# Layer 0 of a graph network on one core: order of the last chunks, filler products in PE's waits, a fifth search behind the scaling, and one gather for the last tile's neighbours

## The chip, the cores and the metric

The kernel runs on one core of a Trainium2 chip. The metric is the device time of one execution in microseconds. The engines are named as the profile names them: PE multiplies matrices (its weight loads are PEld), DVE does vector work, ACT activations and copies, POOL issues the gathers, SP issues most transfers.

## The reference, cut to what matters

Four layers work on x (2708 nodes, 128 features) and a weighted adjacency matrix adj (2708 x 2708, fp32). The change is in layer 0:

```python
def _lap_mul(A, x):
    d = 1.0 / jnp.sqrt(jnp.sum(A, axis=-1))
    return d[:, None] * (A @ (d[:, None] * x))
...
z = _lap_mul(A, x) @ W1 + b1
z = jax.nn.leaky_relu(z, negative_slope=0.1)
sq = jnp.sum(z * z, axis=-1)
d2 = sq[:, None] + sq[None, :] - 2.0 * (z @ z.T)
d2 = jnp.maximum(d2, 0.0)
S = jnp.exp(-jnp.sqrt(d2 + 1e-10) / (2.0 * sigma))
S = jnp.where(ranks < k, S, 0.0)   # the k = 4 nearest nodes of each row
A2 = S + A
out = _lap_mul(A2, x) @ W2 + b2
...
h = jnp.maximum(_layernorm(x, axis=-1), 0.0)
x = x + _L0_gnn_ref(h, adj, L0_gnn_W1, L0_gnn_b1, L0_gnn_W2, L0_gnn_b2, 1, 4)
```

So layer 0 multiplies by adj twice, once with the degrees of adj, and once with those of adj plus a sparse matrix of four neighbours a row. Layers 1 to 3 (attention, a mean aggregation, a plain one) follow with the new x.

## The kernel before, in words

**Tiles and chunks.** The nodes are cut into 22 tiles of 128 rows (T = 22), the last of 20 (TAIL), in six groups of four (GROUPS). adj lies transposed in DRAM. A chunk is 128 of its rows by 2708 columns, 1354 KB, the last 20 rows by 2708, 212 KB. `chunk(i)` (L80 to L90) loads chunk i by a transfer on SP's queue into one of the four buffers of the pool "big", or, for the last five (L0_RES = 5: chunks 17 to 21), into slots res17 to res21 of the pool "rows", where they stay. A product over all nodes is six column blocks, five of 512 and one of 148, in six PSUM tiles acc0 to acc5. PE does an fp32 product in two passes, so a chunk makes 12 records.

**Stage 1, sums** (loop at L366 to L381). While chunks 0 to 21 stream in, PE sums the columns of each with a 32-column matrix of ones (L373), and between them, in `weighted` (L335 to L362), transposes the normalised x and multiplies it by W1 and W2. The sums become degrees and their inverse roots (L382 to L406), which scale y1 (L410).

**Stage 2, aggregation 1** (`aggregate`, L272 to L316). For each streamed chunk, six column blocks times y's tile (`product`, L284); the resident chunks come last, block by block, and after each block `done` uses the result. The last 20 rows are loaded three times more at other partitions (`last_rows`, L92 to L99).

**Stage 3, strips** (L504 to L535). For each tile PE makes z times z transposed, with the squares added by a bf16 product (L520); ACT copies each PSUM tile to a strip of 128 x 2708 in SBUF (L527); DVE finds the eight largest of each row (`max`, L529) and their places (`max_index`, L531). For the last four tiles (LATE = T - 4) the places are put off (`find_last`, L547): two of their strips live in the slots U and Z of the pool "lay", two in "big". Then the distances of the four nearest become similarities on ACT and DVE, new degrees and dinv2 (L552 to L569), and y2 is scaled, tile by tile, by DVE and ACT (L574 to L579) and written to DRAM (ydr) in two parts of 11 tiles (L581 to L586). Behind that on DVE stand the four put-off searches (L590), and `row_numbers` (L541), which turns places into rows of ydr (near_u).

**Stage 4, aggregation 2 and neighbours** (L748 to L758). `add_near` (L600 to L617) does, for each tile and each of the four neighbours, an indirect gather on POOL of 128 rows of ydr into one of 23 buffers, and on DVE a term: gathered rows times the similarity, added to xs. Tiles 0 to 14 are recorded ahead of aggregation 2, tiles 15 to 19 in `done_l0` (L733) after group results, tiles 20 and 21 at the end. Aggregation 2 on y2 keeps chunks 13 to 16 in their buffers (kept=4). The tail adds the last tiles' terms, normalises the last group and goes on to layer 1.

**What sets the order.** Each engine runs its instructions in one order. A scheduler places what isn't pinned (`pin`), pools decide which buffer a tile gets, and a transfer or a writer waits until the buffer's last reader has finished. Transfers on SP and ACT take one of eight lanes in turn, and a transfer waits for the one before it on its lane. Transfers on SP are pinned to program order, so one that waits holds up those behind it.

Of the kernel before, what the change touches and what calls it, by code (L numbers as in the profile page):

```python
# [9 lines left out]
F32 = mybir.dt.float32  # L10
U32 = mybir.dt.uint32
BF16 = mybir.dt.bfloat16
AF = mybir.ActivationFunctionType
ALU = mybir.AluOpType
# [4 lines left out]
P = 128  # L19
TOPK = 4  # L20
# [5 lines left out]
def kernel(  # L26
# [18 lines left out]
    nc = tc.nc  # L45
    N, D = x.shape
    assert D == P
    T = -(-N // P)
    TAIL = N - (T - 1) * P
    KBS = [(k0, min(512, N - k0)) for k0 in range(0, N, 512)]  # L50
    NKB = len(KBS)
    GROUPS = [(t, min(t + 4, T)) for t in range(0, T, 4)]
    L0_RES = 5
    TAIL_RES = 6

    def width(t):
        return TAIL if t == T - 1 else P
# [8 lines left out]
    lay = ctx.enter_context(tc.tile_pool(name="lay", bufs=1))  # L66
# [3 lines left out]
    ps_s = ctx.enter_context(tc.tile_pool(name="ps_s", bufs=2, space=PSUM))  # L70
    ps_a = ctx.enter_context(tc.tile_pool(name="ps_a", bufs=1, space=PSUM))

    def pin(ins):

        return tc.keep_in_program_order(ins)

    resident = {}
# [24 lines left out]
    def spread(y, queue):  # L102

        for g in range(1, 4):
            queue.dma_start(y[32 * g : 32 * g + TAIL, T - 1, :], y[:TAIL, T - 1, :])
# [4 lines left out]
    res_rows = rows_open.enter_context(tc.tile_pool(name="rows", bufs=1))  # L110
    pools.update(res=res_rows, n=L0_RES)
    xs = keep.tile([P, T, D], F32, name="xs")
# [9 lines left out]
    ident = consts.tile([P, P], F32, name="ident")  # L122
# [25 lines left out]
    with nc.allow_non_contiguous_dma(reason="256 elements"):  # L148
# [3 lines left out]
    ident_b = consts.tile([P, P], BF16, name="ident_b")  # L152
# [20 lines left out]
        out=tri, in_=ones_b, pattern=[[-1, P]], compare_op=ALU.is_ge, fill=0.0, base=0, channel_multiplier=1  # L173
# [23 lines left out]
    def acc(b):  # L197
        return ps_a.tile([P, 512], F32, name=f"acc{b}")

    def span(g):  # L200
        return slice(GROUPS[g][0] * P, min(GROUPS[g][1] * P, N))

# [69 lines left out]
    def aggregate(y, done, more=None, kept=0, back=1, first=1):  # L272

        out = [acc(b) for b in range(NKB)]
        last = T - pools["n"]

        def product(i, b):
            k0, n = KBS[b]
            r = slice(32 * (b % 4), 32 * (b % 4) + TAIL) if i == T - 1 else slice(0, P)
            nc.tensor.matmul(  # L284
                out[b][:, :n],
                y[r, i, :],
                chunk(i)[r, k0 : k0 + n],
                start=(i == 0),
                stop=(i == T - 2),
            )  # L290

        for i in range(last):
            if more is not None:
                more(i)
            resident[i] = chunk(i)
            if i > 2 and T - 1 in resident and pools["apart"]:
                last_rows()
            for b in range(NKB):
                product(i, b)
            if i < last - kept:  # L300
                del resident[i]
            if i >= back and (i - back) % 2 == 0:
                absent = [j for j in range(last, T) if j not in resident]
                for j in absent[: first if i == back else 1]:
                    chunk(j)
        if more is not None:
            for i in range(last, T):
                more(i)
        for b in range(NKB):
            product(T - 1, b)  # L310
        for b in range(NKB):
            for i in range(last, T - 1):
                product(i, b)
            if b:
                done(b - 1, out)
        done(NKB - 1, out)  # L316

    NG = len(GROUPS)
# [5 lines left out]
    res = l0.enter_context(tc.tile_pool(name="l0_res", bufs=1))  # L324
# [10 lines left out]
    def weighted(g, part):  # L335
        t0, t1 = GROUPS[g]
        if part == 0:
            p = acc(g % 2)
            for t in range(t0, t1):
                o = (t - t0) * P  # L340
                mm = nc.tensor.transpose(
                    p[:, o : o + width(t)], h0[: width(t), t, :], ident[: width(t), : width(t)]
                )
                if t == t0:
                    pin(mm)
            nc.scalar.copy(h0T[:, span(g)], p[:, : span(g).stop - span(g).start])
            return
        dst, w = ((y1, w1), (hw2, w2))[part - 1]
        p = acc(2 * part + g % 2)
        for t in range(t0, t1):  # L350
            o = (t - t0) * P
            mm = nc.tensor.matmul(
                p[: width(t), o : o + P], h0T[:, cols(t)], w, start=True, stop=True
            )
            if t == t0:
                pin(mm)
        for a, e, n in ((t0, min(t1, T - 1), P), (max(t0, T - 1), t1, TAIL)):
            if a < e:
                (nc.scalar.copy, nc.vector.tensor_copy)[part - 1](
                    dst[:n, a:e, :],  # L360
                    p[:n, (a - t0) * P : (e - t0) * P].rearrange("p (t f) -> p t f", f=P),
                )  # L362

    for g in range(NG):
        layernorm_relu(h0, g)
    for i in range(T):  # L366
        c = chunk(i)
        w = width(i)
        if 3 <= i < 3 + 3 * NG:
            weighted((i - 3) // 3, i % 3)  # L370
        for b, (k0, n) in enumerate(KBS):
            g = 32 * (b % 4)
            nc.tensor.matmul(  # L373
                sums[b // 4][g : g + 32, :n],
                ones[:w, :32],
                c[:w, k0 : k0 + n],
                start=(i == 0),
                stop=(i == T - 1),
            )
        if i < FIRST:  # L380
            del resident[i]  # L381
    sum_rows = lay.tile([P, 1024], F32, name="sum_rows", tag="U")  # L382
    for half, p0, p1 in ((0, 0, 128), (1, 0, 32 * (NKB - 5)), (1, 32 * (NKB - 5), 32 * (NKB - 4))):
        n = KBS[4 * half + p0 // 32][1]
# [3 lines left out]
    for g0, g1 in [(0, 4)] + [(b, b + 1) for b in range(4, NKB)]:  # L388
# [3 lines left out]
        for c in range(min(4, e - 4 * g0)):  # L392
            w = min(width(4 * b + c) for b in range(g0, g1))
# [84 lines left out]
    p = ps_s.tile([P, 512], F32, name="ps")  # L478
    pin(nc.tensor.transpose(p[:, :P], wg, ident))
    nc.vector.tensor_copy(wgT, p[:, :P])  # L480
    p = ps_s.tile([P, 512], F32, name="ps")
# [10 lines left out]
    top_v = res.tile([P, T, 8], F32, name="top_v")  # L492
    top_i = res.tile([P, T, 8], U32, name="top_i")

    LATE = T - 4
    strips = []
    nc.vector.memset(top_v[:, T - 1, :], 0.0)

    def strip(t):
        if LATE <= t < LATE + 2:  # L500
            return lay.tile([P, N], F32, name=f"strip{t}", tag="UZ"[t - LATE])
        return big.tile([P, N + 1], F32, name="strip", tag="big")[:, :N]

    for t in range(T):  # L504
        w = width(t)
# [3 lines left out]
        for bs in (range(4), range(4, NKB)):  # L509
            for b in bs:  # L510
                k0, n = KBS[b]
# [5 lines left out]
            for b in bs:  # L517
                k0, n = KBS[b]
                g = 32 * (b % 4)
# [4 lines left out]
                    start=False,  # L524
                    stop=True,
# [12 lines left out]
    near_u = res.tile([P, T, TOPK], U32, name="near_u")  # L538
# [28 lines left out]
    dinv2 = keep.tile([P, T], F32, name="dinv2")  # L567
    nc.scalar.activation(deg2s, deg2s, AF.Ln)
    nc.scalar.activation(dinv2, deg2s, AF.Exp, scale=-0.5)  # L569
    y2 = lay.tile([P, T, D], F32, name="y2", tag="Y")  # L570
    ydr = dram.tile([P * T, D], F32, name="ydr")
    for i in range(2):
        resident[i] = chunk(i)
    for t0, t1 in ((0, T // 2), (T // 2, T)):  # L574
        for t in range(t0, t1):
            if t % 5 in (1, 3):
                scaled = nc.scalar.mul(y2[:, t, :], hw2[:, t, :], dinv2[:, t : t + 1])
            else:
                nc.vector.tensor_scalar(  # L579
                    y2[:, t, :], hw2[:, t, :], dinv2[:, t : t + 1], None, op0=ALU.mult  # L580
                )  # L581
        pin(
            nc.sync.dma_start(
                ydr.rearrange("(p t) f -> p t f", t=T)[:, t0:t1, :], y2[:, t0:t1, :]
            )
        )  # L586
    with tc.issue_after(scaled.ins):
        nc.scalar.preload_act_table_set("sqrt_and_others")
    for t in (T - 2, T - 1, *range(LATE, T - 2)):
        find_last(t)  # L590
# [4 lines left out]
    simd = res.tile([P, T, TOPK], F32, name="simd")  # L595
    nc.vector.tensor_tensor(
        simd, sim, dinv2[:, :, None].to_broadcast([P, T, TOPK]), ALU.mult
    )

    def add_near(t, late=False):  # L600
        w = width(t)
        for k in range(TOPK):
            g = res.tile([P, D], F32, name="gath", bufs=23)
            nc.gpsimd.indirect_dma_start(  # L604
                out=g[:w, :],
                out_offset=None,
                in_=ydr[:, :],
                in_offset=bass.IndirectOffsetOnAxis(ap=near_u[:w, t, k : k + 1], axis=0),
            )
            term = nc.vector.scalar_tensor_tensor(  # L610
                xs[:w, t, :],
                g[:w, :],
                simd[:w, t, k : k + 1],
                xs[:w, t, :],
                op0=ALU.mult,
                op1=ALU.add,
            )  # L617
            if late and k == 0:
                pin(term)
# [127 lines left out]

    for t in range(15):  # L748
        add_near(t)
    aggregate(y2, done_l0, lambda i: spread(y2, nc.sync) if i == 4 else None, kept=4)  # L750
    transposed(hT, h1, NG - 2, nc.scalar.copy)
    column_terms(NG - 3)
    for t in range(GROUPS[-1][0], T):
        add_near(t, late=True)
    layernorm_relu(h1, NG - 1)
    last_row = last_terms(NG - 1)
# [248 lines left out]
    p = acc(0)  # L1005
# [94 lines left out]
    for t in range(T):  # L1100
# [3 lines left out]
        for b, (k0, n) in enumerate(EKBS):  # L1104
            p = acc(b)
# [272 lines left out]
```

## Time and profile before

| What | us |
|---|---|
| Median of five runs | 1286.74 |
| The five runs | 1278.62, 1291.21, 1277.50, 1289.09, 1286.74 |
| Profiled execution: its time | 1287.12 |
| Profiled execution: span, first to last instruction | 1285.3 |
| PE busy in the span | 1055.8 (82%) |
| Mean granted PE clock | 0.902 of full |
| Stage 1 ends (first product of aggregation 1) | 93.39 |
| Strips: PE | 205 to 327.5 |
| First product of aggregation 2 | 337.06 |
| First and last gather of the long run of gathers | 343.99 and 448.1 |
| Aggregation 2 ends | 528 |
| Layer 0 ends | about 552 |

The page shows the span in 40 slices of 32 us, each digit a tenth of busy time; PEclk is the clock that PE was granted. In the groups, the number after the second bar is how long the engine stood idle just before, and what ended it; "issue" means that the profile shows nothing that it waited for. In a timeline a row has start, duration, engine, line, operation, and idle time before it in brackets. Some matmul records are missing, a few in a hundred.

### The profile page before, as it was taken

Reading aid. Unit: us, or ns where it says so; the run is one execution under the profiler, and the core shown is the slowest. Engines: PE = TensorE matmul, PEld = TensorE weight load, DVE = VectorE, ACT = ScalarE, POOL = GpSimd, SP = SyncE. Lnnn points to the kernel's source line nnn. Section 1 sums busy time; section 2 is a strip of 40 time slices with the busy share of each in tenths; the row PEclk is TensorE's granted clock in tenths of the full one; section 3 lists DMA queues with packets and bytes.
Section 4 is the critical chain, followed back from the end, with each engine's and each line's share of the span. In section 5 each row is a group of like instructions: output and inputs, shape, how many; then the busy total and the mean of one; then the engine's idle time right before and its main releaser. Section 6 shows DMA issues by size and latency. Waiting matters only on the chain. (4 is left out here: it accounts for less than half of the span.)

```text
span 1285.3 us, 10181 instructions
## 1 busy us (share of the span) xinstructions
PE 1055.8 (82%) x3603; PEld 498.4 (39%) x3603; DVE 561.0 (44%) x1177; ACT 410.2 (32%) x636; POOL 243.5 (19%) x211
## 2 busy tenths in 40 slices
PE   3879999999763379798677861787879999999998
PEld 1324444444220134454333430333334445545444
DVE  2020026999932001783566663899970022104003
ACT  3100014544300000475567744687840012003000
POOL 4000000000277700134211103576500000000000
PEclk9989999999875579778899996688889999999999
DMA  9997800001553361256999986999949945761841
GB/s 339 421 388 281 302 2 1 1 1 43 209 206 96 94 247 56 90 226 253 270 401 397 346 360 255 422 422 418 417 180 400 334 162 185 263 244 56 307 157 43
DMA packets 38801, 298.76 MB, mean 232 GB/s; under 512 B 6736, under 2 KB 9711, under 8 KB 12291
## 3 DMA queue, kind: packets, MB, share of 16 engines
q1 hardware_dynamic: 24798, 203.76, 42.0%
q0 software_dynamic: 13952, 94.36, 19.6%
q8 instruction: 28, 0.46, 0.1%
q14 instruction: 23, 0.18, 0.0%
HBM read 265.76 MB, written 32.87 MB: 232 GB/s over the span
## 5 line engine op out<-in xcount | busy, mean ns | idle before, releaser
L284 PE MATMUL acc<-chunk,y 128*128 128x512 f32 (+1 forms) x408 | 180.7, 592 | 74.1 <-issue 59.4
L1213 PE MATMUL acc<-hi,xw 128*128 128x512 f32 (+3 forms) x264 | 123.9, 633 | 57.8 <-DVE hi L1203 57.8
L1106 PE MATMUL acc<-mov,wt 128*128 128x512 f32 (+1 forms) x264 | 115.7, 592 | 40.3 <-DMA mov<-in_adj_dram,src_u 40.0
L284 PE MATMUL acc<-chunk,h 128*128 128x512 f32 (+1 forms) x384 | 148.3, 542 | 0.0
L604 POOL DMA_INDIRECT gath<-ydr,near_u x88 | 83.8, 952 | 337.3 <-DMA ydr<-y 245.8
L284 PEld LDWEIGHTS acc<-chunk,y 128*128 128x128 f32 x408 | 79.3, 204 | 175.4 <-issue 164.5
L512 PE MATMUL acc<-zT 128*128 128x512 f32 (+2 forms) x264 | 112.7, 559 | 0.4 <-ACT strip L527 0.3
L1213 PEld LDWEIGHTS acc<-hi,xw 128*128 128x128 f32 (+1 forms) x264 | 55.5, 219 | 126.2 <-issue 66.0
L1110 DVE COPY mov<-acc 2x512 f32<-2x512 f32 x126 | 74.1, 611 | 59.9 <-PE acc L1106 59.5
L284 PEld LDWEIGHTS acc<-chunk,h 128*128 128x128 f32 x384 | 68.6, 190 | 73.2 <-issue 73.1
L1106 PEld LDWEIGHTS acc<-mov,wt 128*128 128x128 f32 x264 | 52.1, 205 | 103.5 <-issue 91.1
L527 ACT COPY strip<-acc 128x512 f32<-128x512 f32 (+2 forms) x132 | 60.7, 556 | 61.0 <-issue 35.8
L284 PE MATMUL acc<-chunk,attended 128*128 128x512 f32 x192 | 73.1, 542 | 1.2 <-DMA chunk<-in_adj_dram 1.2
L1111 ACT COPY knots<-acc 128x512 f32<-128x512 f32 x88 | 50.5, 590 | 62.1 <-DVE mov L1110 54.1
L1145 POOL DMA_INDIRECT lo<-table,lo_u x22 | 56.1, 2549 | 71.8 <-issue 41.5
L1195 ACT ACTIVATE hi<-hi,lam 128x2708 f32<-128x2708 f32 (+3 forms) x24 | 56.5, 2363 | 34.7 <-issue 25.3
L1191 DVE SCALAR_TENSOR_TENSOR hi<-lo,lam,hi 128x2708 f32<-128x2708 f32 (+3 forms) x24 | 67.1, 2801 | 1.0
L1203 DVE SCALAR_TENSOR_TENSOR hi<-row_all,inv_s,hi 128x2708 f32<-128x2708 f32 (+3 forms) x24 | 67.0, 2797 | 0.4 <-ACT hi L1196 0.4
L512 PEld LDWEIGHTS acc<-zT 128*128 128x128 f32 (+1 forms) x264 | 45.0, 185 | 51.7 <-issue 41.9
L529 DVE MAX8 top_v<-strip 128x8 f32<-128x2708 f32 (+1 forms) x22 | 64.4, 2967 | 0.4 <-ACT strip L527 0.4
L650 ACT COPY u2T<-acc 128x512 f32<-128x512 f32 (+1 forms) x6 | 3.2, 532 | 168.2 <-PE acc L284 168.1
L1196 ACT ACTIVATE hi<-hi,hb 128x2708 f32<-128x2708 f32 (+3 forms) x24 | 56.5, 2361 | 0.7
(281 smaller groups left out, 1177.2 us busy)
## 6 DMA issues: line engine op xcount, KB each, us to landing
chunk<-in_adj_dram SPq DMA_DIRECT2D x108, 1354.0 KB
table<-knots SPq DMA_DIRECT2D x20, 1354.5 KB
res<-in_adj_dram SPq DMA_DIRECT2D x9, 1354.0 KB
chunkY<-in_adj_dram SPq DMA_DIRECT2D x2, 1354.0 KB
chunkU<-in_adj_dram SPq DMA_DIRECT2D x2, 1354.0 KB
res<-in_adj_dram SPq DMA_DIRECT2D x8, 211.6 KB
ydr<-y SPq DMA_DIRECT2D x2, 704.0 KB
gath<-ydr,near_u POOLq DMA_INDIRECT x88
```

What stands on the lines that cost most here:

```text
L284: nc.tensor.matmul(out[b][:, :n], y[r, i, :], chunk(i)[r, k0 : k0 + n], start=(i == 0), stop=(i == T - 2),)
L512: mm = nc.tensor.matmul(zz[b][:w, :n], zT[:, cols(t)], zT[:, k0 : k0 + n], start=True, stop=False)
L527: copied = nc.scalar.copy(s[:w, k0 : k0 + n], zz[b][:w, :n])
L529: nc.vector.max(top_v[:w, t, :], s[:w, :])
L604: nc.gpsimd.indirect_dma_start(out=g[:w, :], out_offset=None, in_=ydr[:, :], in_offset=bass.IndirectOffsetOnAxis(ap=near_u[:w, t, k : k + ...
L1106: nc.tensor.matmul(p[:, :n], wt[:, t, :], moving[t][:, k0 : k0 + n], start=True, stop=True)
L1110: nc.vector.tensor_copy(moving[t + 1][:2, k0 : k0 + n], p[:2, :n])
L1191: nc.vector.scalar_tensor_tensor(num, lo[:w, c], kap, num, op0=ALU.mult, op1=ALU.add)
L1195: nc.scalar.activation(num, num, AF.Ln, scale=sc)
L1196: nc.scalar.activation(num, num, AF.Exp, scale=-1.0, bias=hb40[:w, t : t + 1])
L1203: nc.vector.scalar_tensor_tensor(att[:w, c], row_all[:w, c], inv_s[:w, t : t + 1], att[:w, c], op0=ALU.max, op1=ALU.mult,)
L1213: nc.tensor.matmul(py[b][:, :n], xw[:w, t, :], att[:w, k0 : k0 + n], start=(t == T - 1), stop=(t == T - 2),)
```

## The change

Six edits, all in layer 0.

1. The sums take chunks 0 to 19, then 21 (20 rows), then 20. The transfers on SP change places in the same way.
2. A function `warm(p, n)` issues n bf16 products of 128 x 512 whose result nobody reads. Three follow each of the last six chunks of the sums, into acc0; sixteen stand after the strips and ahead of aggregation 2, into acc5. In PE's order the sixteen come directly behind the last strip's products, and wait only for ACT's copies of acc5.
3. LATE = T - 5: tile 17's search is put off too. Its strip takes the slot of the resident chunk 17, so aggregation 2 loads that chunk again, behind chunk 7's load on SP (back=7). That load waits for the search of strip 17. DVE has five searches in place of four behind y2.
4. ydr is written in three parts, of 9, 8 and 5 tiles.
5. The 4 x 20 neighbours of the last tile are gathered at once: eight copies of 20 x 1 on ACT's queue lay their row numbers and similarities out on four groups of partitions (near_p, simd_p), one gather of 128 rows fetches them, and a product on PE with four_w (sums of blocks of the identity, scaled by simd_p) adds the four groups up; DVE adds the result to xs. 85 gathers in place of 88. On POOL this gather is the 81st, ahead of tile 20's four; on DVE the scaling of four_w stands behind the 32nd of the 60 terms that go ahead of aggregation 2's group results. ACT's eight copies stand behind its table load after y2.
6. In the tail tile 21 goes ahead of tile 20.

The diff, cut to its core:

```diff
+    def warm(p, n):
+        for _ in range(n):
+            pin(
+                nc.tensor.matmul(
+                    p, ident_b, ident_b[:, None, :].to_broadcast([P, 4, P]), start=True, stop=True
+                )
+            )
...
-    for i in range(T):
+    for n_, i in enumerate([*range(T - 2), T - 1, T - 2]):
...
-                start=(i == 0),
-                stop=(i == T - 1),
+                start=(n_ == 0),
+                stop=(n_ == T - 1),
...
+        if n_ >= T - 6:
+            warm(acc(0), 3)
...
-    LATE = T - 4
+    LATE = T - 5
...
-        if LATE <= t < LATE + 2:
-            return lay.tile([P, N], F32, name=f"strip{t}", tag="UZ"[t - LATE])
+        if t == LATE:
+            i = T - L0_RES
+            del resident[i]
+            return res_rows.tile([P, N + 1], F32, name=f"strip{t}", tag=f"res{i}")[:, :N]
+        if LATE < t < LATE + 3:
+            return lay.tile([P, N], F32, name=f"strip{t}", tag="UZ"[t - LATE - 1])
...
+    warm(acc(5), 16)
...
-    for t0, t1 in ((0, T // 2), (T // 2, T)):
+    for t0, t1 in ((0, 9), (9, 17), (17, T)):
...
+    near_p = res.tile([P, 1], U32, name="near_p")
+    simd_p = res.tile([P, 1], F32, name="simd_p")
...
+    for k in range(TOPK):
+        for dst, src in ((near_p, near_u), (simd_p, simd)):
+            nc.scalar.dma_start(dst[32 * k : 32 * k + TAIL, :], src[:TAIL, T - 1, k : k + 1])
+    four_w = res.tile([P, 32], F32, name="four_w")
+    nc.vector.tensor_tensor(four_w, ident[:, 0:32], ident[:, 32:64], ALU.add)
+    nc.vector.tensor_tensor(four_w, four_w, ident[:, 64:96], ALU.add)
+    nc.vector.tensor_tensor(four_w, four_w, ident[:, 96:128], ALU.add)
...
+        if t == T - 1:
+            g = gathered(near_p)
+            nc.vector.tensor_scalar(four_w, four_w, simd_p, None, op0=ALU.mult)
+            p = ps_s.tile([P, 512], F32, name="ps")
+            nc.tensor.matmul(p[:TAIL, :P], four_w[:, :TAIL], g, start=True, stop=True)
+            nc.vector.tensor_tensor(xs[:TAIL, t, :], xs[:TAIL, t, :], p[:TAIL, :P], ALU.add)
+            return
...
-    aggregate(y2, done_l0, lambda i: spread(y2, nc.sync) if i == 4 else None, kept=4)
+    aggregate(y2, done_l0, lambda i: spread(y2, nc.sync) if i == 4 else None, kept=4, back=7)
...
-    for t in range(GROUPS[-1][0], T):
+    for t in reversed(range(GROUPS[-1][0], T)):
```

More of the change, by code (lines that the diff above doesn't have):

```diff
@@ L365 @@
         layernorm_relu(h0, g)
[L366 removed]
+    for n_, i in enumerate([*range(T - 2), T - 1, T - 2]):
         c = chunk(i)
         w = width(i)
[L369 to L370 removed]
+        if 3 <= n_ < 3 + 3 * NG:
+            weighted((n_ - 3) // 3, (n_ - 3) % 3)
         for b, (k0, n) in enumerate(KBS):
@@ L598, with gathered @@
     )
-    def add_near(t, late=False):
-        w = width(t)
-        for k in range(TOPK):
[L603 to L609, printed above, removed]
+    near_p = res.tile([P, 1], U32, name="near_p")
+    simd_p = res.tile([P, 1], F32, name="simd_p")
+    nc.vector.memset(near_p, 0)
+    nc.vector.memset(simd_p, 0.0)
+    for k in range(TOPK):
[5 more added lines that the diff above has]
+    nc.vector.tensor_tensor(four_w, four_w, ident[:, 96:128], ALU.add)
+    def gathered(idx):
+        g = res.tile([P, D], F32, name="gath", bufs=23)
+        nc.gpsimd.indirect_dma_start(
+            out=g[: idx.shape[0], :],
+            out_offset=None,
+            in_=ydr[:, :],
+            in_offset=bass.IndirectOffsetOnAxis(ap=idx, axis=0),
+        )
+        return g
+    def add_near(t, late=False):
+        if t == T - 1:
[5 more added lines that the diff above has]
+            return
+        for k in range(TOPK):
+            g = gathered(near_u[:, t, k : k + 1])
             term = nc.vector.scalar_tensor_tensor(
[L611 to L614, printed above, removed]
+                xs[:, t, :],
+                g,
+                simd[:, t, k : k + 1],
+                xs[:, t, :],
                 op0=ALU.mult,
```

## The prediction, made before the changed kernel ran

> **What bounds the kernel now.** I read the page's slices first, then its costliest groups, a table of stages by windows, and the timelines at the seams that the diff touches. From the page:
>
> ```profile
> PE   3879999999763379798677861787879999999998
> PEclk9989999999875579778899996688889999999999
> DMA  9997800001553361256999986999949945761841
> ...
> L284 PE MATMUL acc<-chunk,y 128*128 128x512 f32 (+1 forms) x408 | 180.7, 592 | 74.1 <-issue 59.4
> L604 POOL DMA_INDIRECT gath<-ydr,near_u x88 | 83.8, 952 | 337.3 <-DMA ydr<-y 245.8
> ```
>
> PE is near full except in slices 10 to 16 (320 to 550 us). The two aggregations on L284 waited 59.4 us for "issue", for nothing that the profile names. The table of windows (us, busy us and records of each engine, granted clock, DMA share, GB/s) places it:
>
> ```profile
> 80.00:84.70 4.70, 2.29 (x16) 0.65 (x8) 0.48 (x2) 0.00 (x0) 0.00 (x0) 1.00 1.00 270
> 84.70:90.00 5.30, 5.26 (x24) 0.95 (x24) 0.65 (x1) 0.00 (x0) 0.00 (x0) 0.68 1.00 412
> 93.40:100.00 6.60, 6.60 (x10) 2.83 (x11) 2.63 (x5) 0.00 (x0) 1.57 (x3) 0.61 0.63 220
> ...
> 327.50:337.00 9.50, 0.00 (x0) 0.00 (x0) 7.77 (x12) 2.82 (x10) 0.00 (x0) 0.67 0.27 109
> 337.00:344.00 7.00, 6.93 (x13) 3.23 (x14) 7.00 (x17) 3.75 (x10) 0.01 (x1) 0.72 0.66 232
> 344.00:368.00 24.00, 23.99 (x64) 11.18 (x62) 12.96 (x29) 0.00 (x0) 18.26 (x19) 1.00 0.85 332
> 368.00:412.00 44.00, 13.98 (x17) 4.40 (x16) 12.21 (x35) 0.00 (x0) 33.29 (x36) 0.54 0.31 86
> 412.00:456.00 44.00, 14.98 (x18) 4.82 (x17) 2.73 (x8) 0.00 (x0) 27.59 (x29) 0.50 0.32 106
> ```
>
> The reader is to see four seams: a DMA dip to 270 GB/s at 80; clocks of 0.68 and 0.61 after it; PE empty from 327.5 to 337 while DVE searches; and from 368 to 456 only 35 products in 88 us, with DMA a third busy and POOL gathering throughout. In the PE timeline the products of the last stretch stand 2.8 us apart, though 76 of them ran in 31.4 us just before:
>
> ```profile
> 337.06 31.38 PE L284 MATMUL acc<-chunk,y 128*128 128x512 f32 x76 [9.60 <-DVE y L579]
> ...
> 400.49 1.01 PE L284 MATMUL acc<-chunk,y 128*128 128x512 f32 x1 [1.78 <-issue]
> 403.29 1.01 PE L284 MATMUL acc<-chunk,y 128*128 128x512 f32 x1 [1.80 <-issue]
> ```
>
> I call this the slow stretch. 35 products at 0.41 us are some 14 us of the 88, so it costs about 74 us. SP's waits there are named "remote": PE's releases of chunk buffers reach it late as well.
>
> ```profile
> SPq L87 <- remote: 83.0, 3, 33.2
> ```
>
> Its cause isn't in the profile. In time it goes with POOL: gathers run back to back, 0.95 us plus 0.30 of gap, from 343.99 to 448, and PE is quick again from 456. The burst is 83 gathers: 60 whose terms DVE adds at once (done at 421), and 23 that fill the buffers. So whatever moves the first gather moves the end of the stretch, and whatever PE does before the stretch is kept.
>
> **The change part by part**, against the profiled execution (1287.1 us; the median of five runs is 1286.7, its range 1277.5 to 1291.2).
>
> 1. *Order of the last chunks, three unread products after each of the last six.* Before:
>
> ```profile
> 79.64 1.90 PE L373 MATMUL ps<-res,ones 128*32 128x512 f32 x12 [0.61 <-DMA res<-in_adj_dram]
> 84.74 5.38 PE L373 MATMUL ps<-res,ones 128*32 128x512 f32 x24 [2.45 <-DMA res<-in_adj_dram]
> ```
>
> Twelve records take 1.90 us at full clock; the last 24 took 5.38, 1.6 over, as the clock had dropped while PE waited for chunk 20. It landed at 84.7 (5.1 us after chunk 19 instead of 3.25), the 20 rows at 86.1. The bytes stay the same, so with the order turned round the full chunk lands between 84.7 and 86.1 and is followed by one set of 1.90 us and three unread products. Those: a strip tile takes 5.58 us, its twelve fp32 passes 4.55 of that, so 2708 bf16 columns take 1.03 and 512 take 0.2 us; 0.6 per chunk. In the busiest of these rounds PE then has 1.90 + 1.16 + 0.6 = 3.7 us against 3.25 of load, a lag under 1 us that the lighter rounds after it make good. The sums end at 88 to 89 instead of 90.1: -1.2. The first aggregation ran at half clock from 92.0 to 98.9, some 5.5 us of its own work, 2.7 lost; the products end only 1.5 us nearer to it, so I take half of that, -1.5. Together **-2.7**, ends 0 (the load still lands at 86.1 and the clock drops anyway) and -4.5. After it PE is continuous to 180, so it is kept.
>
> 2. *One more search put off.* Each search is 2.97 us plus 0.08 on DVE, which lags ACT at the end of the strips:
>
> ```profile
> 331.18 2.96 DVE L529 MAX8 top_v<-strip 20x8 f32<-20x2708 f32 x1
> ...
> 339.35 2.97 DVE L549 FIND_INDEX8 top_i<-top_v,strip 128x8 uint32<-128x2708 f32 x1
> ```
>
> ACT's last strip copy ends at 328.7, so the last maximum can start 2.5 us earlier, not 3.05: **-2.5**, ends 0 and -3.05. The search comes back after y2: five there instead of four, first term of DVE at about 3 us later against y2. That is covered: 23 buffers are 23 x 1.25 = 29 us of gathers. Chunk 17 is loaded once more (1354 KB, 3.25 us) behind chunk 7 on SP; in the windows from 368 DMA is at a third, so 0. If that cover went it is at most 3.25 us.
>
> 3. *Sixteen unread products ahead of aggregation 2.* They wait for ACT's last strip copy: 328.7 on before's clock, 16 x 0.2 = 3.2 us, end 331.9, and the first y2 product comes at 337.06 - 2.5 = 334.6. PE stood at half clock from 330.96 to 341.2, 3.5 us after its last product; of that, 4.1 us was work, so 2.07 us was lost. The new gap is 2.7 us, under 3.5: the clock stays. At half clock they take 6.4 us and end at 335.1: 0.5 late. I take -2.07, ends +0.5 and -2.07. The page "TensorE: Matmul & The Clock Gate" of the Trainium skill (Part 1) has the clock fall after an idle window of about 3.4 us, the window running freely; the row's 3.5 agrees. By a free-running window a gap of 2.7 us could now and then still fall in one: without the gain of the clock the sum would be -6.1 in place of the -8.2 below.
>
> 4. *y2 to DRAM in three parts.* The two parts were issued at 338.26 and 339.49 and landed at 341.4 and 343.1, the first gather came at 343.99. With a smaller last part I take **-0.8** for the first gather, ends 0 and -1.5. SP's one more issue stands ahead of chunk 2's, half a microsecond that the next loads hide.
>
> 5. *Last tile's neighbours in one gather.* Eight copies of 20x1 on ACT's queue, which was idle from 340.8 to 506. Three such 20-row copies took SP 2.44 us to issue at 344.3, so eight are 6.5 us. They wait for near_u (354 on the old clock) and for lanes last used by chunks 2 to 4 and the spread, all issued by 347. So they land near 362; DVE's scaling of four_w, which stands after 32 of the 60 terms, comes at about 344 + 32 x 1.25 = 384, the gather as number 81. Hidden: 0. The rule against this step is in "DMA: Bandwidth & Descriptors" of the Trainium skill (where the ~2 us goes): a fixed cost of about 2 us for each DMA however small. Eight in a row would be 16 us by it, as an estimate, and still be in time: the sum is the same by both. The burst remains 83 gathers (85 in all instead of 88). In the tail eight terms of 0.34 us become four, a product and an add: **-0.9**, ends 0 and -1.5.
>
> **Sum.** The first gather, and so the end of the slow stretch, comes 2.7 + 2.5 + 0.8 = 6.0 us earlier. PE starts 5.2 earlier and gains 2.07 of clock, so it has 2.07 - 0.8 = 1.3 us more work done when the gathers start: -1.3. Tail -0.9. In all -8.2: **1279 us**, with its own range 1273 to 1287 (the ends of the terms).
>
> **The rivals.** *The slow stretch shrinks.* Its cause is unknown and it's worth 74 us, so a change of phase between gathers, terms and loads can move it by far more than the sum. For it: its start (PE's releases are prompt at 353, 19 us late at 357) lies close to DVE's first term, which moves; against it: the same burst of 83 remains. A third of it gone gives 1279 - 25 = 1254. *Nothing arrives*: what PE gains at the seams is lost in the stretch, because it ends with another thing than the burst: 1287. *Slower*: DVE is stopped at four_w. If a lane that ACT's small copies wait for is held by a load that waits for one of PE's late releases (in before they came at 377, 410 and 443), simd_p comes late; DVE's 28 terms behind it wait, POOL runs out of buffers at gather 56, at 344 + 55 x 1.25 = 413, and burst and stretch grow one for one. It makes the kernel slower from a landing at 413 + 8 = 421, by 1% from 434; at 443 the time is 1279 + 30 = 1309. Against it: the lanes' earlier users were issued by 347.
>
> **How the numbers follow.** As summed 0.55, stretch shrinks 0.20, nothing arrives 0.11, DVE stopped 0.14. About 1% (12.9 us) is what a measurement of this kernel tells from no change. Faster by more: the shrinking 0.20 and 0.05 of the summed case's lower end. Slower: 0.14 and a hundredth. Within 1%: 0.60. The range 1257 to 1297 leaves out half of the shrinking and most of the stopped case.
>
> **What would show it.** Step 1: chunk 20's set of twelve near 1.9 us and the clock near 1 there. Step 2: first y2 product about 5 us earlier. Step 3: clock 1 from 329 on. Step 4: the first gather under 6.5 us after the first y2 product (6.9 before). Step 5: no wait of DVE for simd_p. The sum fails if the stretch's length, 368 to 456, isn't that of the burst.

## The result, and the profile after

The changed kernel takes 1278.63 us in the median of 42 runs, the kernel before 1282.24 in 79. The ratio is 0.9977 (95% interval 0.9964 to 0.9991), so 2.9 us are gained, between 1.2 and 4.6. The forecast of 1279 names that time, but by luck: it takes a gain of 8.2 from an execution that lay 4.9 us over the median of before. The gain is a third of the sum, as some of its terms failed.

The slices of the changed kernel, and the same group:

```profile
PE   4889999999863389698677870878879999999998
PEclk9999999999985589688899995698889999999999
DMA  9998800001563370265999988999949936762831
...
L294 PE MATMUL acc<-chunk,y 128*128 128x512 f32 (+1 forms) x408 | 175.7, 580 | 64.2 <-issue 57.7
```

The idle time for "issue" is 57.7 us, 59.4 before: the slow stretch is as it was. The table of windows of the changed kernel (columns as before):

```profile
84.00:90.00 6.00, 6.00 (x38) 1.77 (x38) 1.47 (x4) 0.57 (x1) 0.00 (x0) 1.00 1.00 422
92.40:100.00 7.60, 7.60 (x15) 3.37 (x16) 2.64 (x5) 0.00 (x0) 1.58 (x3) 0.78 0.71 222
...
325.70:332.70 7.00, 3.61 (x16) 1.46 (x15) 4.97 (x8) 2.78 (x9) 0.00 (x0) 1.00 0.00 0
332.70:339.50 6.80, 6.75 (x17) 3.21 (x18) 6.80 (x16) 3.73 (x10) 0.00 (x0) 1.00 0.69 238
339.50:368.00 28.50, 26.00 (x69) 12.12 (x67) 16.39 (x31) 0.00 (x0) 21.78 (x23) 1.00 0.94 364
368.00:412.00 44.00, 14.06 (x17) 4.40 (x16) 12.79 (x39) 0.00 (x0) 33.34 (x36) 0.56 0.33 99
412.00:454.00 42.00, 14.27 (x17) 4.63 (x17) 1.73 (x5) 0.00 (x0) 24.22 (x26) 0.50 0.31 94
```

The clock is full at 84 to 90 (0.68 before) and from 325.7 to 368 (0.67 and 0.72 before, in the windows up to 344), and still 0.78 at the start of aggregation 1. From 339.5 to 368 PE is busy for 26.0 of 28.5 us: with the clock up it now waits for chunks. In the PE timeline, the idle time is in brackets:

```profile
326.88 3.61 PE L205 MATMUL acc<-ident_b 128*128 128x512 bf16 x16 [1.26 <-ACT strip L545]
332.75 9.35 PE L294 MATMUL acc<-chunk,y 128*128 128x512 f32 x24 [2.26 <-DVE y L598]
343.83 18.41 PE L294 MATMUL acc<-chunk,y 128*128 128x512 f32 x48 [1.73 <-DMA chunk<-in_adj_dram]
363.01 5.21 PE L294 MATMUL acc<-chunk,y 128*128 128x512 f32 x13 [0.76 <-DMA chunk<-in_adj_dram]
```

Then the tail, first DVE and then PE:

```profile
534.41 0.69 DVE L770 TENSOR_TENSOR own<-row_all,r_nat 128x512 bf16<-128x512 f32 x1 [1.83 <-ACT row_all L742]
538.29 0.28 DVE L649 TENSOR_TENSOR xs<-xs,ps 20x128 f32<-20x128 f32 x1 [3.18 <-PE ps L648]
538.49 0.33 DVE L653 SCALAR_TENSOR_TENSOR xs<-gath,simd,xs 128x128 f32<-128x128 f32 x1
```

```profile
532.64 1.12 PE L739 MATMUL ps<-ident,r_nat 128*128 128x128 f32 x4 [5.22 <-DVE r_nat L730]
533.55 1.71 PE L751 MATMUL acc<-wga,h1T 128*128 128x1 f32 x8
535.12 1.09 PE L261 MATMUL ps<-ident,h 128*128 128x128 f32 x4
536.00 1.71 PE L751 MATMUL acc<-wga,h1T 128*128 128x1 f32 x8
537.64 0.61 PE L648 MATMUL ps<-gath,four_w 128*20 128x128 f32 x2
```

DVE stands idle for 3.18 us, up to 538.29, for the product with four_w (L648). On PE that product stands behind the transposes of r_nat, which wait for DVE, and behind three groups of products; tile 20's four terms stand behind its add on DVE. In the kernel before DVE ran through eight terms from 544.13 without a wait of this kind:

```profile
544.13 1.75 DVE L610 SCALAR_TENSOR_TENSOR xs<-gath,simd,xs 128x128 f32<-128x128 f32 x5
```

Profiles of both kernels were taken twice, so the stages can be compared beyond one execution. In the table, "resident" is the first product of aggregation 2 with the resident 20 rows, "table" the last table load of ACT in layer 0. Times in us.

| stage | before, twice | changed, twice |
|---|---|---|
| start to aggregation 1 | 93.39, 91.61 | 92.40, 92.81 |
| aggregation 1 to last strip product | 234.07, 234.13 | 233.21, 231.52 |
| last strip product to aggregation 2 | 9.60, 9.60 | 7.14, 7.13 |
| aggregation 2 to first gather | 6.93, 6.92 | 6.79, 6.80 |
| first gather to resident | 156.39, 156.22 | 149.87, 154.25 |
| resident to table (tail) | 51.51, 51.48 | 54.82, 54.67 |
| table to the end | 733.4, 729.3 | 730.4, 732.7 |

### The profile page after: what moved, and what is told of

The parts are those of the page before. It is cut to its first block, busy times and chain, and to the rows that moved or that the text cites. A ratio compares the mean times of both kernels' runs of the same rounds, so it can differ in the third digit from the quotient of the medians.

```text
span 1274.6 us, 10268 instructions
## 1 busy us (share of the span) xinstructions
PE 1056.4 (83%) x3639; PEld 501.8 (39%) x3639; DVE 560.5 (44%) x1180; ACT 410.2 (32%) x636; POOL 243.7 (19%) x208
## 5 line engine op out<-in xcount | busy, mean ns | idle before, releaser
L294 PE MATMUL acc<-chunk,y 128*128 128x512 f32 (+1 forms) x408 | 175.7, 580 | 64.2 <-issue 57.7
L1149 PE MATMUL acc<-mov,wt 128*128 128x512 f32 (+1 forms) x264 | 111.2, 575 | 40.9 <-DMA mov<-in_adj_dram,src_u 39.8
L635 POOL DMA_INDIRECT gath<-ydr,near_u x84 | 80.3, 956 | 325.9 <-DMA ydr<-y 242.3
L1017 ACT ACTIVATE sg<-row_all,c_nat 128x2708 bf16<-128x2708 f32 (+1 forms) x22 | 56.3, 2558 | 0.1
```

Source lines behind the costliest of these rows:

```text
L294: nc.tensor.matmul(out[b][:, :n], y[r, i, :], chunk(i)[r, k0 : k0 + n], start=(i == 0), stop=(i == T - 2),)
L635: nc.gpsimd.indirect_dma_start(out=g[: idx.shape[0], :], out_offset=None, in_=ydr[:, :], in_offset=bass.IndirectOffsetOnAxis(ap=idx, axis=0),)
L1149: nc.tensor.matmul(p[:, :n], wt[:, t, :], moving[t][:, k0 : k0 + n], start=True, stop=True)
```

## The experiments

Edits are against the changed kernel. "Ratio" is to the kernel before on the same chip.

**e1_early: the product recorded with the fifth group.**

```diff
-    late = {0: (15,), 1: (16,), 2: (17,), 3: (18, 19), 4: ()}
+    late = {0: (15,), 1: (16,), 2: (17,), 3: (18, 19), 4: (T - 1,)}
-    for t in reversed(range(GROUPS[-1][0], T)):
-        add_near(t, late=True)
+    add_near(T - 2, late=True)
```

> The changed kernel with one move: the last tile's product with four_w and its add to xs are recorded after the fifth group's results instead of in the tail, so that on PE the product stands ahead of the transposes of r_nat that wait for DVE. Theory (the tail ate part of the gain: DVE idles 3.2 us for that product, and tile 20's terms queue behind it): the stretch from the first product with the resident last rows to the last table load falls from 54.8 us to about 50 (51.5 before the change), and the time is 3 to 5 us under the changed kernel's, about 0.6% under the kernel before. Rival (the tail is bound elsewhere, and the small gain of the whole is lost in the slow stretch): that stretch stays within 1 us of 54.8, and the time within 1 us of the changed kernel's.

Measured: ratio 0.9936 (0.9899 to 0.9973), 1273.4 us; tail 48.37 us. PE's product stands at 522.1 and DVE adds its result without a wait:

```profile
526.60 0.24 DVE L649 TENSOR_TENSOR xs<-xs,ps 20x128 f32<-20x128 f32 x1
```

The tail is 6.4 us shorter than in the changed kernel and 3.1 shorter than before. The theory holds: the one gather is a gain, and its product's place took more than that away. The evidence is the tail; the ratios of this kernel and the changed one overlap.

**e2_four: four gathers of 20 rows and four terms again, tile 20 first.** It takes out near_p, simd_p, four_w and the branch for the last tile, and with the order of tiles 20 and 21 also edit 6.

> The changed kernel with the last tile's neighbours gathered as before (four gathers of 20 rows, four terms, tile 20 ahead of tile 21; no small copies, no four_w). Theory (tail): the stretch from the first product with the resident last rows to the last table load goes back to about 51.5 us, and the time is some 3 us under the changed kernel's. Rival (the small copies and the one gather are free, as forecast, or gain 0.9 us): the time is equal or about 1 us higher than the changed kernel's.

Measured: ratio 0.9956 (0.9930 to 0.9982), 1276.29 us; tail 51.35 us, as before the change. So the one gather as built, together with edit 6, costs 3.4 us in the tail.

**e3_after_again, e4_before_again: both kernels unedited once more.**

> The changed kernel once more, for a second profile of its stages. Theory: the seams ahead of the slow stretch repeat within 0.3 us (first product of aggregation 2 at 332.7, first gather 6.8 us later), the tail repeats (54.8 us), and what differs between executions is the end of the slow stretch and the attention layer. Rival: the tail of 54.8 us is an accident of one execution and comes out nearer to 51.5.

> The kernel before once more, for a second profile of its stages. Theory: first product of aggregation 2 at 337.1 within 0.3 us, tail of 51.5 us again; the end of the slow stretch differs by some us between executions, which is why two profiles differ by 10.7 us where the medians differ by 3.6. Rival: the stages repeat as they were to the end of layer 0, and the difference between profile and median lies in the later layers alone.

Measured: 1281.63 and 1281.15 us, one run each; the stages are in the table above. The tails repeat within 0.2 us. The seam of searches and the way to the first gather repeat within 0.02. Two things vary: the first product of aggregation 2 came at 331.46 and 335.34 (I had expected 332.7 and 337.1, within 0.3), and "first gather to resident" differs by 4.4 us in the changed kernel. In the kernel before that stage repeats, against my theory; its two executions differ by 1.8 us in the first stage and by 4.1 behind layer 0. The second execution of before shows where the 1.8 come from: the last 24 records took 3.73 us, not 5.38, as the clock had not fallen.

```profile
84.61 3.73 PE L373 MATMUL ps<-res,ones 128*32 128x512 f32 x24 [2.42 <-DMA res<-in_adj_dram]
```

**e5_no_unread: without the unread products.**

```diff
-            warm(acc(0), 3)
+            pass
-    warm(acc(5), 16)
```

> The changed kernel without the unread products (both the three after each of the last six chunks and the sixteen ahead of aggregation 2). Theory (they keep the clock up at both seams): clock half again in the first 4 to 6 us of either aggregation; first product of aggregation 1 to last strip product longer by 1 to 2 us (231.5 to 233.2 with them, 234.1 before the change); first gather to first product with the resident last rows some 2 to 4 us longer (about 152 with them, 156.3 before); the time 3 to 5 us above the changed kernel's. Rival (what the clock gains is taken back in the slow stretch, since that ends with the gathers): first gather to resident rows stays within the spread of the executions, 150 to 154, and the time is at most 2 us above.

Measured: ratio 1.0030 (1.0004 to 1.0056); the changed kernel's interval ends at 0.9991, so from ratio to ratio the unread products are a gain of some 0.5%, 7 us, with the two kernels measured on different occasions. Its one profile shows less: first gather to resident 155.0 us, against 149.9 and 154.3, and 1.7 us more to the end of layer 0 than the mean of the two profiles of the changed kernel. Where the rest of the 7 us lies isn't shown. The clock was at half for 10.24 us from 326.88, as in the kernel before. Aggregation 1 to last strip product is 233.2, no longer than with them. And at the first seam the three products are a loss. Without them:

```profile
85.42 1.90 PE L384 MATMUL ps<-res,ones 128*32 128x512 f32 x12 [0.25 <-DMA res<-in_adj_dram]
87.30 1.53 PE L408 MATMUL acc<-ident,sum_rows 128*128 128x128 f32 x10
```

With them, in the changed kernel:

```profile
84.26 1.90 PE L384 MATMUL ps<-res,ones 20*32 20x512 f32 x12
86.09 0.82 PE L205 MATMUL acc<-ident_b 128*128 128x512 bf16 x3
86.85 1.90 PE L384 MATMUL ps<-res,ones 128*32 128x512 f32 x12
88.68 0.82 PE L205 MATMUL acc<-ident_b 128*128 128x512 bf16 x3
89.44 1.16 PE L408 MATMUL acc<-ident,sum_rows 32*128 32x32 f32 x10
```

Without them PE starts on chunk 20 as soon as it has landed, at 85.4. In the changed kernel it has landed at 85.8, but PE comes to it at 86.85, and the last three unread products stand between the sums and the transposes that wait for them. The sums end at 87.3 without them and at 88.75 and 89.16 with them. When chunk 20 lands differs between executions, so the better count is from there: the transposes start 1.9 us after it without the unread products, 3.6 and 3.8 with them. Aggregation 1 starts at 90.6, not at 92.4 and 92.8.

**e6_old_order: chunks 20 and 21 in the old order.**

```diff
-    for n_, i in enumerate([*range(T - 2), T - 1, T - 2]):
+    for n_, i in enumerate(range(T)):
```

> The changed kernel with the sums taking the chunks in the old order (20, then 21), unread products kept. Theory (the order of the last chunks is worth nothing, since the bytes are the same and the start of aggregation 1 came at 92.4 to 93.4 with the new order and 91.6 to 93.4 with the old): first product of aggregation 1 at 91.6 to 93.4 again, time within 1 us of the changed kernel's. Rival (the order gains the 1.2 us that was forecast): the first product comes 1 us or more later than 93.4.

Measured: ratio 1.0006 (0.9977 to 1.0035), which overlaps the changed kernel's; aggregation 1 starts at 93.25, inside the spread that the kernel before shows by itself. The order is worth under 1 us in these profiles; the ratios leave between nothing and some 8 us open. In this profile the clock fell at chunk 20, after a wait of 1.83 us and with the unread products in place, and its twelve records took 3.36 us instead of 1.90:

```profile
83.47 3.36 PE L384 MATMUL ps<-res,ones 128*32 128x512 f32 x12 [1.83 <-DMA res<-in_adj_dram]
```

e1, with the new order, shows the same at chunk 19, after a wait of 2.66 us. Of the eleven profiles with the unread products these are the two in which the clock fell at the last chunks.

**e7_quarter: one gather per tile for tiles 0 to 14.**

```diff
-            g = gathered(near_u[:, t, k : k + 1])
+            g = gathered(near_u[:, t, k : k + 1]) if k == 0 or t >= 15 else g
```

> The changed kernel with one gather per tile instead of four for tiles 0 to 14; all four terms of such a tile read the same gathered rows, so it leaves out 45 gathers and three of four neighbours there. 38 gathers run back to back in place of 83, some 48 us. Theory (the slow stretch is tied to the run of gathers and ends with it): it ends about 56 us earlier, by 400, PE's idle time put down to issue falls from about 57 us to 10 to 25, and aggregation 2 ends 35 to 50 us earlier. Rival (it is tied to something else, as PE's own products, chunk loads or DVE's terms): idle time for issue stays above 45 us.

Measured: 1215.3 us in one run. The waits of PE for issue from 300 to 560 us (total, times, longest; the changed kernel has 55.9 us there), then its timeline:

```profile
PE acc L294 <- issue: 9.5, 7, 2.2
```

```profile
380.74 1.01 PE L294 MATMUL acc<-chunk,y 128*128 128x512 f32 x1 [1.09 <-issue]
382.15 1.01 PE L294 MATMUL acc<-chunk,y 128*128 128x512 f32 x1 [0.40 <-issue]
383.56 3.37 PE L294 MATMUL acc<-chunk,y 128*128 128x512 f32 x5 [0.41 <-issue]
```

The stretch ends at 380.7, 43.7 us after the first gather, and first gather to resident falls to 95.4 us. 45 gathers fewer are worth some 57 us. The unbroken run was of 33 gathers, not of the 38 expected: POOL paused for 4.6 us behind the 33rd, at 379.2, and the last five of the 38 came in a second run. The stretch belongs to the gathers; DVE's terms were all there.

**e8_rows16: gathers and terms of 16 rows.** `near_u[:16, ...]` in the gather, and the first 16 rows in the term.

> The changed kernel with gathers of 16 rows instead of 128 for all tiles but the last, terms on these rows only, so it leaves out the neighbours of the other 112 rows of each tile. The run of 83 gathers stays, an eighth of its rows and bytes moved. Theory (PE's slow products go with the number of gather instructions: 67 PE instructions to 65 gathers recorded from 368 to 456): the stretch stays, idle for issue 45 us or more. Rival (they go with the rows or bytes that the gathers move, or their descriptors): idle for issue falls under 20 us and aggregation 2 ends 40 us or more earlier, even if POOL still takes about 1.25 us a gather.

Measured: 1277.74 us in one run, idle for issue 56.7 us. POOL took 0.84 us a gather plus 0.30 and had issued the 83rd by 431.8, 95.1 us after the first; PE was quick again only at 449.0, 112.3 us after it:

```profile
447.60 0.40 PE L294 MATMUL acc<-chunk,y 128*128 128x148 f32 x1 [1.69 <-issue]
449.00 7.55 PE L294 MATMUL acc<-chunk,y 128*128 128x512 f32 x12 [1.00 <-issue]
```

So at these sizes neither the rows nor the bytes matter, nor the time that POOL takes to issue; what is left is the number of gathers. The end of the stretch, counted from the first gather: 111.1 and 112.4 us in the two profiles of before, 112.2 to 114.4 in the six of the changed kernel and its versions with 83 gathers in the run, and 43.7 with 33. That is 1.32 to 1.38 us a gather.

**e9_self, e10_self_8, e11_8: fewer gathers, and a shorter run.** All three contain the edit of e1. A node's nearest neighbour is itself, so its term can read y2's tile (e9, e10); 8 buffers instead of 23 keep POOL from running far ahead of DVE's terms (e10, e11).

```diff
-            g = gathered(near_u[:, t, k : k + 1])
+            g = gathered(near_u[:, t, k : k + 1]) if k else y2[:, t, :]
...
-        g = res.tile([P, D], F32, name="gath", bufs=23)
+        g = res.tile([P, D], F32, name="gath", bufs=8)
```

> The changed kernel with the early product, and without gathers for the nearest of the four neighbours: a node's distance to itself is zero, so its first neighbour is itself, and the term reads y2's own tile. 64 gathers in all, all in one run, in place of 85 with 83 in the run. Theory (the slow stretch ends some 1.35 us times the number of gathers in the run after the first one: 83 gave 112 to 114 us, 38 gave 47): it ends about 88 us after the first gather, 26 us sooner, first gather to resident rows about 128 us, and the time is 25 to 30 us under that of the early product, some 1246. Rival (from a run of this length on PE is bound by something else, chunk loads for one): under 12 us gained.

> As the run without gathers for the node itself, with 8 gather buffers in place of 23, so that POOL can run only 8 gathers ahead of DVE's terms: the run is 45 + 8 = 53, and the other 11 gathers go in small groups among aggregation 2's group results. Theory (only the unbroken run slows PE, and small groups cost it nothing, as the first 20 gathers cost nothing): another 11 x 1.35 = 15 us gained on the run with 23 buffers, some 1231. Rival (the deferred gathers slow PE later by as much, or DVE's late terms then wait for them): within 4 us of the run with 23 buffers, or slower.

> The changed kernel with the early product and 8 gather buffers in place of 23, all neighbours gathered: the run is 60 + 8 = 68, the other 17 gathers follow in small groups. Theory (as above): 15 x 1.35 = 20 us gained on the early product with 23 buffers, some 1253. Rival (deferred gathers cost as much later): within 4 us of the early product's 1273.

| kernel | run of gathers | end of the stretch after the first gather | idle for issue | us | ratio |
|---|---|---|---|---|---|
| e1_early | 83 | 113.0 | 57.4 | 1273.4 | 0.9936 (0.9899 to 0.9973) |
| e11_8 | 68 | 92.0 | 39.9 | 1253.0 | 0.9779 (0.9745 to 0.9814) |
| e9_self | 64 | 89.9 | 40.8 | 1246.1 | 0.9736 (0.9695 to 0.9777) |
| e10_self_8 | 8 + 45 | 71.4 | 18.2 | 1223.3 | 0.9559 (0.9531 to 0.9586) |

Expected were 1246 for e9, 1253 for e11 and 1231 for e10. (What e9's expectation says of e7, 38 gathers and 47 us, is by the trace 33 and 43.7.) The length of the run sets the loss. The deferred gathers take little of it back: the tail is 48.4 us in e1 and e9, 48.6 in e10, and 50.8 in e11, where all neighbours are gathered. e10 gains 8 us more than the rule gives. Its first slow product comes only at 386.2, 49 us after the first gather, where the kernels with 23 buffers show it after 26 to 33:

```profile
372.08 11.62 PE L294 MATMUL acc<-chunk,y 128*128 128x512 f32 x29 [2.65 <-DMA chunk<-in_adj_dram]
384.04 0.59 PE L294 MATMUL acc<-chunk,y 128*128 128x512 f32 x1 [0.34 <-issue]
386.15 0.59 PE L294 MATMUL acc<-chunk,y 128*128 128x512 f32 x1 [1.52 <-issue]
```

Its run has a pause of 2.2 us after the eighth gather, where POOL waits for DVE's first term. The pause alone isn't the reason: e11 has one of 1.6 us at the same place, and its slow products start after 34 us. The cause stays open.

**e12_self_4: e10 with 4 buffers.**

> As the run with 8 buffers and no gathers for the node itself, with 4 buffers: the run is 45 + 4 = 49, and 15 gathers follow among the group results. Theory (length of the unbroken run alone): another 4 x 1.35 = 5 us gained, some 1218. Rival (with 4 buffers a gather waits for the term of the fourth before it, and DVE's late terms wait for gathers): the run takes longer than 1.25 us a gather, or the tail grows over 48.6 us, and the time is equal or above 1223.

Measured: 1190.81 us, but on this occasion the kernel before took 1190.13 (17 runs, 1185 to 1197), 90 us less than on every other; ratio 1.0012 (0.9989 to 1.0034). The question about 4 buffers stays open, since the profile has no slow stretch at all. Nor does it have the run of 49 gathers that was expected: POOL waited for DVE after every few, 7.2 us after the first four, and its longest unbroken run is of 16. PE's timeline:

```profile
341.95 27.50 PE L294 MATMUL acc<-chunk,y 128*128 128x512 f32 x72 [1.84 <-DVE top_i L567]
370.93 41.13 PE L294 MATMUL acc<-chunk,y 128*128 128x512 f32 x108 [1.47 <-DMA chunk<-in_adj_dram]
411.99 9.04 PE L294 MATMUL acc<-res,y 20*128 20x512 f32 x28
```

First gather to resident is 74.4 us, 82 less than in the kernel before (the prediction put the stretch at 74): aggregation 2 at PE's own pace. With runs so short this profile alone could be the work of the edit. The kernel before, which has its run of 83, wasn't profiled on this occasion, but it was faster by 90 us, somewhat more than those 82. That makes it likely that the stretch needs the gathers, but also something that isn't in the kernel: e5 to e8 ran on the same chip, some twelve minutes earlier, with times of before near 1281 and with the stretch. On this occasion e12 as a whole gains nothing on the kernel before; PE waits 6.4 us in it for the gather of near_p. All ratios above, the change's own too, are from occasions with the stretch.

## Why the prediction was right or wrong

The sign came out as forecast, and the median by luck; the gain of 8.2 did not. (The low end, 1273, isn't what the prediction's terms give: their ends add up to 1276.) By its steps, with the two profiles of each kernel:

1. *Order and the first unread products, -2.7.* Mis-sized, and one premise fell. The sums ended where the step put them, at 88.75 and 89.16, but the kernel before ends them at 88.34 when its clock doesn't fall, so the start of aggregation 1 moved by nothing that the kernel's own spread of 1.8 us would let one see. Aggregation 1 to the last strip product is shorter by 1.7 (means 234.1 and 232.4). That is time at half clock: of aggregation 1, 5.2 us ran at half clock in both profiles of before, 3.4 and none in those of the changed kernel. The unread products aren't shown to be the cause, since e5 without them has 3.4 too. The step that failed is "a lag under 1 us that the lighter rounds after it make good": the unread products of the last two chunks have no load to hide behind. By e5 they make the sums end 1.4 to 1.8 us later, and the transposes start 1.7 to 1.9 us later after chunk 20's landing. The clock drop there, which the step meant to cure, is in one of the two profiles of before only, and e1 and e6 have it in spite of the products.
2. *The put-off search, -2.5.* Right: 9.60 to 7.14, 2.46 us. The last maximum waits 0.33 us for ACT, as worked out. The second load of chunk 17 was issued at 358.7 and hidden.
3. *Sixteen unread products, -2.07, and step 4's share.* They did what was forecast: they took 3.61 us, PE was idle 2.26 us, and the clock stayed full through that gap in all eleven profiles that have them. The reason given, that a gap under 3.5 us keeps the clock, is not enough. In three of the eleven (the second of the changed kernel, e7 and e11) the clock fell at the next wait, one of 1.9 to 2.3 us for a chunk. In the changed kernel's second execution (one row of PE's timeline, then two windows with the columns of the tables above):

```profile
342.93 23.11 PE L294 MATMUL acc<-chunk,y 128*128 128x512 f32 x55 [2.12 <-DMA chunk<-in_adj_dram]
```

```profile
340.23:343.64 3.41, 1.29 (x5) 0.68 (x4) 3.41 (x3) 0.00 (x0) 2.50 (x4) 1.00 1.01 426
343.64:347.05 3.41, 3.41 (x5) 1.35 (x4) 3.41 (x3) 0.00 (x0) 2.59 (x3) 0.50 1.04 391
```

The spell at half clock lasted 3.41 us here, and 10.24 us in the kernel before, from 330.66 to 340.90 (the prediction has these ends, as those of the half clock in step 1, some 0.3 us late, so it cost 1.92 us and not 2.07). Spells of 3.41 us and its multiples agree with the window of about 3.4 us on the Trainium skill's page "TensorE: Matmul & The Clock Gate" (Part 1). That page has the clock fall after an idle window; here PE was busy for 1.29 us of the window ahead of the fall. For the -1.3 that the sum puts down to PE's head start when the gathers begin, the means of first gather to resident show -4.2 (156.3 and 152.1), with a spread of 4.4 us, of which the spell above is 1.7. The 149.9 of the first profile is the lowest: e1, e2 and e6, which keep the sixteen products and all 83 gathers, have 152.3 to 154.8, and the mean with them is 153.1, so -3.2. What brings more than the clock isn't settled. Part of what the clock gained went at once into waits for chunks (1.73 and 0.76 us).
4. *y2 in three parts, -0.8.* Mis-sized: 0.13 us. The three parts went out one behind the other at some 400 GB/s and the last landed 6.2 us after y2's first scaling, 6.4 before. Only the start of the first part had moved, by 0.2 us. A smaller last part doesn't help where the parts queue.
5. *One gather, -0.9 in the tail.* Wrong in sign: +3.25. The copies were hidden as forecast (issued from 350.2 to 357.0, 0.73 us for most of them on ACT, so 6.8 us in all and not the 16 of the estimate), DVE never waited for simd_p, and the burst stayed at 83. What failed is "eight terms of 0.34 us become four, a product and an add", which counts the product by its duration and not by where it stands in PE's queue. e1 and e2 show both halves: the one gather gains 3 us on the kernel before, the place of its product costs 6.4.

Sum of the stages' means: -1.6 to the last strip product (0.1 and -1.7), -2.5, -0.1, -4.2 and +3.2, so -5.2 to the end of layer 0 (-4.2 with the mean of five profiles under 3), against a gain of 2.9 (1.2 to 4.6) by the ratio; two profiles of each, with 4 us between two of the same kernel, can't do better.

The rivals: the slow stretch did not shrink in the changed kernel. That on e12's occasion it seems to have been absent for the kernel before as well is not the change of phase that this rival spoke of. DVE was not stopped at four_w, but a wait of the same kind, for the product made with it, was there in the tail. That the end of the stretch goes with the burst holds by the number of gathers, not by POOL's time (e8).

## What to carry to other kernels

Price a product that is added to an engine by what stands ahead of it in that engine's order, not by its duration: one of 0.6 us cost 6.4 here, and moving its record a few lines gave that back. Work that fills an idle engine is free only while the load it hides behind is there; the last portion of it lies on the path. Where an engine is slow for nothing that it waits for, find what else runs in that time and vary its number, size and pace one by one: e7, e8 and e11 found 1.35 us a gather in a stretch that the profile calls "issue", and led to a kernel 4.4% faster than the one before (e10) by a few edited lines more. And take the reference's time again on every occasion: one showed 90 us less for the same program.

## What the runs showed of the hardware

- While an unbroken run of indirect gathers is under way, PE passes about one instruction per 1.4 us (products 2.8 us apart, one weight load between them), from 26 to 34 us after the first gather (49 in e10) until 1.32 to 1.41 us times their number after it, whether a gather has 16 rows or 128. PE's releases reach SP late by as much as 77 us: the product of chunk 5 ended at 366.4 in the kernel before, the load that waited for it was issued at 443.2.
- The trace itself is thinner on the occasions with the stretch. In the kernel before it holds 116 of the 1328 semaphore updates with which the 83 gathers landed (16 each), in e12, without the stretch, all 1024 of 64. A path for such updates that is full, and that PE's own would share, would fit. No run shows this path, and the five gathers after the stretch, when PE was quick, left only 18 of 80, so it stays a conjecture.
- On one occasion the kernel before took 90 us less, as it would without the stretch. What differs from the others isn't known.
- PE's granted clock changed on a grid of 3.41 us, and the length of a wait alone doesn't tell whether it falls: it fell after waits of 1.83 (e6), 2.12 (the changed kernel's second profile) and 2.45 us (before), and stayed full through 2.26 (the changed kernel) and 2.42 us (before's second profile). What the fourteen profiles do show: no window of this grid in which PE was busy for less than 41% was followed by one at full clock.
- A gather's time on POOL hardly depends on its rows: 0.84 us for 16, 0.95 for 128, with 0.30 between two.
